# A second level of Strassen's form inside three of the seven aggregation products of a graph layer

## The chip, the core and the metric

The kernel runs on one core of one Trainium2 chip. The metric is device time in microseconds (us) of one execution; lower is better. Engines are named as the profile names them: PE is TensorE (matmuls), PEld its weight loads, DVE is VectorE, ACT is ScalarE, POOL is GpSimd, and SP is SyncE, which here only issues DMAs.

## The reference

Two graph layers over `x` (8 batches, 2048 nodes, 256 features) and one matrix `adj` (2048 x 2048), all in fp32. The change lies in the first product of the first layer, `agg`:

```python
# layer 0
A_norm = adj + eye(2048)
dinv = rsqrt(A_norm.sum(0) + A_norm.sum(1) - diagonal(A_norm))
A_hat = A_norm * dinv[:, None] * dinv[None, :]
agg = einsum('nm,bmd->bnd', A_hat, x)              # 8 x 2048 x 256
h = relu(batchnorm(agg.reshape(-1, 256) @ W1.T + b1))   # 256 -> 512
out = batchnorm(h @ W2.T + b2)                     # 512 -> 256
x = layernorm(x + out)
# layer 1: attention with 4 heads, masked where adj == 0
q, k, v = split(x @ W)
x = layernorm(x + softmax(q @ k.T / 8 + mask) @ v)
```

## The kernel before

**Aggregation as seven products.** Let A be `adj` plus the identity, turned so that the contracted node lies on the partitions. Columns of A are cut into chunks of 512 output nodes: `k` (0 or 1) names a pair of chunks, one in each half of the nodes. For one `k`, `T[k, (i, j)]` is the block of contracted half i and output half j, held as 128 x 8 x 512 (8 blocks of 128 contracted nodes). On the other side `S[v, i, j]` is `x` of batch b+i, contracted half j, and 128 of the 256 features (`d` is 0 or 1), held as 128 x 8 x 128. Two batches by two halves times two halves by two halves is a 2 x 2 block product. It is done in Winograd's variant of Strassen's form, with seven products in place of eight. The sums and differences of operands are called `S[v, 1]` to `S[v, 4]` (functions `s1` to `s4`) and `T[k, 2]` to `T[k, 4]` (`t2` to `t4`); `T[k, (0, 1)]` is overwritten with its own difference to `T[k, (0, 0)]`.

**Units.** The loop at L453 runs over 16 units `v = (k, b, d)`: two k, four pairs of batches, two halves of the features. A unit is seven calls of `product` (L360), each of 8 matmuls of 128 x 128 weights by 512 columns into one of four PSUM buffers of pool `psa`. The order on PE is p1, p6, p2, p7, p4, p5, p3. Each product is read from PSUM and added into a quarter of `ag` (tiles ag00, ag10, ag11, ag01; the first index is the batch, the second the half of output nodes); p1 is copied by ScalarE, the others are added by VectorE, and each finished quarter is multiplied by `dbc` (dinv of the output nodes) on GpSimd.

**What goes beside it.** While unit v runs, the next unit's `S` tiles are loaded by SP (`load_form`, L169), multiplied by dinv on GpSimd (`scale`, L333) and combined on GpSimd (`s1` to `s4`). The tiles are called forms; class `Form` hands out nine names, and `product` gives the name back after its last use. At the turn from k=0 to k=1 new `T` blocks are fetched from scratch memory, and VectorE makes the mask of zeros (`mask_of`, L186), `T[k, (0, 1)]`'s difference and t2 to t4.

**Linear layer.** After both d of a pair of batches, `linear` (L404) multiplies `ag` of one batch by W1, again with seven products (PSUM pool `psh`, matmul L412). Their operands `G[i, 1]` to `G[i, 4]` come from `linear_form` (L402) on GpSimd, partly in place in `ag`. Results go into tiles h0 and h1, then to scratch memory `h_d`, and VectorE takes batch norm statistics of them. `linear` for batch 1 of the pair follows the unit directly; for batch 0 it is put into a list `later`, which is run in the next unit just after p1.

**Order.** The whole stage is under a manual schedule: each engine executes its instructions in the order in which the Python code issues them. An instruction that waits holds up everything behind it on its engine.

**After it** come the last four chunks' linear layer (L678), the second linear layer (L633), and attention (L945 to L986), which takes most of the span.

Of the kernel before, what the change touches and what calls it, by code (L numbers as in the profile page):

```python
# [26 lines left out]
def tile_gcn_then_masked_attention(  # L27
# [102 lines left out]

    HT = NT // 2
    NK = HT // TPC
    CHUNKS = ((0, 0), (1, 0), (1, 1), (0, 1))
# [18 lines left out]
        T[1, ij] = quarter(4 + s)  # L154


    free = [f"x{i}" for i in range(9)]

    class Form:
        def __init__(self):  # L160
# [6 lines left out]
    def load_form(b, j, d):  # L167
        f = Form()
        nc.sync.dma_start(  # L169
            f.t,  # L170
            x[b, j * HT * P : (j + 1) * HT * P, d * P : (d + 1) * P].rearrange(
                "(t p) d -> p t d", p=P
            ),
        )
        return f

    def mask_out(k, ij, m8):
        i, j = ij
        c0 = (j * NK + k) * CH
        nc.sync.dma_start(mask_d[:, i * HT : (i + 1) * HT, c0 : c0 + CH], m8)  # L180

    def mask_of(k, ij):

        i, j = ij
        m8 = bp.tile([P, HT, CH], U8, name="m8")
        nc.vector.tensor_scalar(m8, T[k, ij], 0.0, None, op0=ALU.is_equal)  # L186
        if i == j:
            for q in range(TPC):
                m = k * TPC + q
                nc.vector.tensor_copy(  # L190
                    m8[:, m, q * P : (q + 1) * P], mdiag[:, i * HT + m, :]
                )
        mask_out(k, ij, m8)
# [4 lines left out]
    with tc.tile_pool(name="bt7", bufs=1, side="right") as bp7, tc.tile_pool(  # L198
# [4 lines left out]
        engines=ALL4  # L203
    ):
        T[1, HALVES[3]] = quarter(7, bp7)
        m8 = bp.tile([P, HT, CH], U8, name="m8")
        rsum = sp1.tile([P, NT], F32, name="rsum")
        diag = sp1.tile([P, NT], F32, name="diag")

# [87 lines left out]
        diagonal()  # L297
        first_t1(nc.vector, slice(2 * P, CH))
        mask_out(0, (0, 1), m8)

    lp = right.enter_context(
        tc.tile_pool(name="l0", bufs=1, side="right", reuse_waits="tile")
# [1 line left out]
    with tc.tile_pool(  # L304
        name="psa", bufs=4, space=PSUM
    ) as psa, tc.tile_pool(name="psh", bufs=4, space=PSUM) as psh, tc.manual_schedule(engines=ALL4):
        for j in range(2):
            lp.tile([P, NH, CH], F32, name=f"h{j}")
        w1f = lp.tile([P, 4, H // 2], F32, name="w1f")
        dbc = []  # L310

# [48 lines left out]
        def product(s, t):  # L360
            pa = psa.tile([P, CH], F32, name="pa")
            for m in range(HT):
                nc.tensor.matmul(  # L363
                    pa, s.t[:, m, :], t[:, m, :], start=(m == 0), stop=(m == HT - 1)
                )
            s.done()
            return pa
# [5 lines left out]
        def t3(k, slot):  # L373
            T[k, 3] = quarter(slot)
            nc.vector.tensor_sub(T[k, 3], T[k, 2], T[k, (0, 0)])
# [5 lines left out]
        def fetch(k, ij, slot):  # L381
            T[k, ij] = quarter(slot)
            nc.sync.dma_start(T[k, ij], bt_d[HALVES.index(ij)])
# [20 lines left out]
        def linear(k, b, ag, i):  # L404

            cs = [(b + i) * NCH + j * NK + k for j in range(2)]
            lo, hi = (lp.tile([P, NH, CH], F32, name=f"h{j}") for j in range(2))

            def products(w, t):
                for s in range(2):  # L410
                    ph = psh.tile([P, CH], F32, name="ph")
                    nc.tensor.matmul(ph, W1[w][:, s * P : (s + 1) * P], t, start=True, stop=True)  # L412
                    yield s, ph

            def plus(h, f, p, u):
                nc.vector.scalar_tensor_tensor(
                    h[:, f, :], p, b1s[:, f : f + 1], u, op0=ALU.add, op1=ALU.add
                )

            for s, p in products((0, 0), ag[i, 0][:, 0, :]):  # L420
                nc.scalar.copy(lo[:, 2 + s, :], p)  # L421
            linear_form(ag, i, 3)
            for s, p in products((0, 1), ag[i, 0][:, 1, :]):
                plus(lo, s, p, lo[:, 2 + s, :])
            linear_form(ag, i, 4)
            for s, p in products(2, G[i, 2]):
                nc.vector.tensor_add(hi[:, s, :], p, lo[:, 2 + s, :])
            for s, p in products(3, G[i, 3]):
                nc.vector.tensor_add(hi[:, 2 + s, :], p, hi[:, s, :])
            for s, p in products((1, 1), G[i, 4]):  # L430
                plus(lo, 2 + s, p, hi[:, 2 + s, :])
            nc.sync.dma_start(h_d[cs[0]], lo)
            for s, p in products(1, G[i, 1]):
                plus(hi, 2 + s, p, hi[:, 2 + s, :])
                nc.vector.tensor_add(hi[:, s, :], p, hi[:, s, :])
            for s, p in products(4, ag[i, 1][:, 1, :]):
                plus(hi, s, p, hi[:, s, :])
            nc.sync.dma_start(h_d[cs[1]], hi)
            for c, h in zip(cs, (lo, hi)):
                for f in range(NH):  # L440
                    nc.vector.bn_stats(st1[:, f, c, :], h[:, f, :])

        later = []
        for i, j in ((0, 0), (1, 0), (1, 1), (0, 1)):
# [4 lines left out]
        nc.gpsimd.tensor_sub(W1[2], W1[1], W1[0, 0])  # L449
        nc.gpsimd.tensor_sub(W1[3], W1[0, 0], W1[1, 0])  # L450
        nc.gpsimd.tensor_sub(W1[4], W1[0, 1], W1[2])
        ag = None
        for v, (k, b, d) in enumerate(units):  # L453
            first, last = v == 0, v == len(units) - 1
# [6 lines left out]
            c11, c12, c21, c22 = (ag[ij][:, d, :] for ij in HALVES)  # L461
            u1, u2, u3 = c21, c12, c22

            def do_p6():
                p6 = product(S[v, 2], T[k, 2])
                nc.vector.tensor_add(u2, p6, u1)

            p1 = product(S[v, 0, 0], T[k, (0, 0)])
            for f in later:
                f()  # L470
            later = []
            nc.scalar.copy(u1, p1)  # L472
            if not last:
                nb, nd = units[w][1:]
                S[w, 0, 0] = load_form(nb, 0, nd)
                S[w, 1, 0] = load_form(nb + 1, 0, nd)
                S[w, 1, 1] = load_form(nb + 1, 1, nd)
            if turn:
                fetch(k + 1, (0, 0), 0)
            if first:  # L480
# [4 lines left out]
                t4(0, 6)  # L485
            else:
                do_p6()
            if turn:
                fetch(k + 1, (0, 1), 4)
            p2 = product(S[v, 0, 1], T[k, (1, 0)])  # L490
            nc.vector.tensor_add(c11, p2, u1)  # L491
            nc.gpsimd.tensor_mul(c11, c11, dbc[0][:, 0, :])  # L492
            if first:
                p3 = product(S[v, 4], T[k, (1, 1)])
                do_p6()
            if not last:
                S[w, 0, 1] = load_form(nb, 1, nd)
                for ij in ((0, 0), (1, 0), (1, 1)):
                    scale(w, *ij)
            if turn:  # L500
                fetch(k + 1, (1, 1), 2)
            if d and not last:
                for i in range(2):
                    linear_form(ag, i, 1)
            p7 = product(S[v, 3], T[k, 3])
            nc.vector.tensor_add(u3, p7, u2)
            if turn:
                mask_of(k + 1, (0, 1))
                t1 = T[k + 1, (0, 1)]
                nc.vector.tensor_sub(t1, t1, T[k + 1, (0, 0)])  # L510
            if not (last or turn):
                s1(w)
                s2(w)
                s3(w)
            p4 = product(S[v, 1, 1], T[k, 4])
            nc.vector.tensor_add(c21, p4, u3)
            nc.gpsimd.tensor_mul(c21, c21, dbc[0][:, 0, :])
            if turn:
                fetch(k + 1, (1, 0), 6)
                t2(k + 1, 5)  # L520
            if not last:
                scale(w, 0, 1)
                if not turn:
                    s4(w)
            p5 = product(S[v, 1], T[k, (0, 1)])
            nc.vector.tensor_add(c22, p5, u3)
            nc.vector.tensor_add(u2, p5, u2)
            nc.gpsimd.tensor_mul(c22, c22, dbc[0][:, 1, :])
            if d and not last:
                linear_form(ag, 1, 2)  # L530
            if turn:
                t3(k + 1, 1)
            if not first:
                p3 = product(S[v, 4], T[k, (1, 1)])
            nc.vector.tensor_add(c12, p3, u2)
            nc.gpsimd.tensor_mul(c12, c12, dbc[0][:, 1, :])

            n = v % (len(units) // NK)
            if n in (2, 4, 6):
                mask_of(k, ((0, 0), (1, 0), (1, 1))[n // 2 - 1])  # L540
            if last:
                break
            if d:
                linear(k, b, ag, 1)
                linear_form(ag, 0, 2)
                if turn:
                    t4(k + 1, 3)
                    s1(w)
                    s2(w)
                later = [lambda k=k, b=b, ag=ag: linear(k, b, ag, 0)]  # L550
                if turn:
                    later += [lambda w=w: s3(w), lambda w=w: s4(w)]

# [13 lines left out]

        x0 = []  # L570
        for name, size in (
            ("h1", [P, NH, CH]), ("dbc", [P, 2, CH]), ("w1f", [P, 4, H // 2])
        ):
            t = lp.tile(size, F32, name=name).rearrange("p a b -> p (a b)")
            for i in range(size[1] * size[2] * 2 // N):
                tx = t[:, i * N // 2 : (i + 1) * N // 2].rearrange("p (t d) -> p t d", d=D)
                nc.sync.dma_start(
                    tx, x[0, len(x0) * CH : (len(x0) + 1) * CH].rearrange("(t p) d -> p t d", p=P)
                )
                x0.append(tx)  # L580
        wt = lp.tile([P, NH, CH], F32, name=f"h0")
        w2s = wt[:, :2, :].rearrange("p a b -> p (a b)").rearrange("p (f o) -> p f o", f=NH)
        w2f = wt[:, 2:, :].rearrange("p a b -> p (a b)").rearrange(
            "p (n f o) -> p n f o", n=4, f=2
        )
        nc.sync.dma_start(w2s, w2t.rearrange("(c p) f -> p c f", p=P))
        for n, slot in enumerate((0, 5, 6, 1, 3)):
            read_h(2 + n, slot)

        def w_half(i, j):  # L590
            return w2s[:, 2 * j : 2 * j + 2, i * P : (i + 1) * P]

        W = {ij: w_half(*ij) for ij in HALVES}
        W[1], W[2], W[3], W[4] = (w2f[:, n] for n in range(4))
        nc.gpsimd.tensor_add(W[1], W[1, 0], W[1, 1])
        nc.gpsimd.tensor_sub(W[2], W[1], W[0, 0])
        nc.gpsimd.tensor_sub(W[3], W[0, 0], W[1, 0])
# [753 lines left out]
```

## Time and profile before

| | |
|---|---|
| Median of 3 runs | 3564.32 us (3564.18 to 3565.26) |
| Profiled execution | 3566.12 us, its span 3564.3 us |
| Mean granted PE clock | 0.998 |
| Busy share of the span | PE 99%, DVE 59%, ACT 44%, POOL 65% |
| First and last matmul of the aggregation (L363) | 58.9 and 999.5 us |
| Aggregation matmuls (L363), 1792 records | 774.8 us busy |
| Linear layer inside the stage (L412), 392 records | 76.8 + 76.7 + 26.3 us busy |

Every fp32 matmul shows as two records, so 16 units of seven products of 8 matmuls are 1792 records. A record's duration includes the pipeline: records start closer together than they last, so the pace is read from the starts and not from the mean duration. Busy times of one group are unions and can be added up along one engine.

### The profile page before, as it was taken

The numbers are of one execution on the slowest core, as the hardware profiler recorded it, in microseconds if no ns is written. First come the engines' busy times: TensorE is split into PE (matmuls) and PEld (weight loads), VectorE is DVE, ScalarE is ACT, GpSimd is POOL, SyncE is SP. The second block draws the span as 40 slices with busy tenths as digits, with TensorE's granted clock in tenths as the row PEclk, the third lists the DMA queues.
The fourth block names the chain that finished last, engine by engine and source line by source line (L and its number), as shares of the span: only waits on it lengthen the run. The fifth ranks groups of instructions, "written<-read, shape, count | busy, mean of one in ns | idle before, by whom it ended". The sixth has DMA issues, their size and how long they took to land. (4 is left out here: it accounts for less than half of the span.)

```text
span 3564.3 us, 55375 instructions
## 1 busy us (share of the span) xinstructions
PE 3527.1 (99%) x22483; PEld 1461.0 (41%) x22483; DVE 2113.4 (59%) x3128; ACT 1575.4 (44%) x1952; POOL 2330.5 (65%) x1588
## 2 busy tenths in 40 slices
PE   8999999999999999999999999999999999999998
PEld 5444444444444433433343433343443334343332
DVE  6224343442346656766766776676676676677666
ACT  5000000000045455665665565565566566566555
POOL 4544364435357656777777787777677777777777
PEclk9999999999999999999999999999999999999999
DMA  9122342231256445666575566566656556555655
GB/s 342 54 77 76 95 153 78 71 95 39 84 217 249 156 84 109 128 126 123 110 149 117 115 129 134 113 133 129 118 124 136 114 117 145 115 117 115 122 107 121
DMA packets 197577, 440.16 MB, mean 123 GB/s; under 512 B 14128, under 2 KB 121152, under 8 KB 186944
## 3 DMA queue, kind: packets, MB, share of 16 engines
q0 software_dynamic: 64656, 239.37, 35.3%
q1 hardware_dynamic: 132048, 196.11, 16.2%
q8 instruction: 178, 2.92, 0.3%
q10 hardware_dynamic: 608, 1.06, 0.1%
q14 instruction: 87, 0.71, 0.1%
HBM read 126.62 MB, written 75.51 MB: 57 GB/s over the span
## 5 line engine op out<-in xcount | busy, mean ns | idle before, releaser
L945 DVE SCALAR_TENSOR_TENSOR prob<-mask,st 128x1024 f32<-128x1024 uint8 x1024 | 1239.0, 1215 | 434.6 <-PE st L933 358.6
L951 ACT ACTIVATE prob<-prob 128x1024 f32<-128x1024 f32 x1024 | 1081.2, 1056 | 913.4 <-DVE prob L945 836.6
L963 PE MATMUL out_ps<-prob,v 64*64 64x512 f32 x8192 | 1074.2, 595 | 3.6 <-DVE ot L991 2.6
L933 PE MATMUL st<-qt,kt 64*64 64x512 f32 x8192 | 1062.9, 589 | 0.1
L986 POOL TENSOR_TENSOR acc<-acc,prob 128x1024 f32<-128x1024 f32 x317 | 825.6, 2604 | 5.5 <-DMA prob<-prob 0.6
L363 PE MATMUL pa<-t,x 128*128 128x512 f32 x1792 | 774.8, 594 | 2.8 <-ACT t L239 2.8
L973 POOL DMA_DIRECT2D prob<-prob x447 | 403.6, 928 | 565.4 <-PE out_ps L963 453.4
L933 PEld LDWEIGHTS st<-qt,kt 64*64 64x64 f32 x8192 | 312.5, 133 | 566.7 <-issue 527.0
L363 PEld LDWEIGHTS pa<-t,x 128*128 128x128 f32 x1792 | 341.4, 191 | 432.9 <-issue 428.7
L963 PEld LDWEIGHTS out_ps<-prob,v 64*64 64x64 f32 x8192 | 290.8, 133 | 542.4 <-issue 470.5
L975 POOL TENSOR_TENSOR acc<-acc,prob 128x1024 f32<-128x1024 f32 x126 | 298.1, 2366 | 7.5
L867 PE MATMUL pm<-x1t,wq 128*128 128x512 f32 x512 | 250.8, 613 | 0.7 <-ACT x1t L836 0.7
L492 POOL TENSOR_TENSOR ag<-ag,dbc 128x512 f32<-128x512 f32 x16 | 20.2, 1264 | 314.7 <-DVE ag L491 287.2
L472 ACT COPY ag<-pa 128x512 f32<-128x512 f32 x16 | 9.4, 588 | 450.0 <-PE pa L363 434.0
L421 ACT COPY h<-ph 128x512 f32<-128x512 f32 x28 | 16.4, 585 | 416.7 <-PE ph L412 416.7
L984 POOL TENSOR_TENSOR acc<-prob 128x1024 f32<-128x1024 f32 x64 | 170.7, 2667 | 3.0 <-DMA prob<-prob 3.0
L762 ACT ACTIVATE x<-x,ln_nm,ln_rs 128x256 f32<-128x256 f32 x256 | 137.6, 586 | 7.5 <-POOL ln_nm L758 7.5
L1039 DVE SCALAR_TENSOR_TENSOR x<-pm,ri,x 128x64 f32<-128x64 f32 x512 | 109.6, 277 | 43.6 <-PE pm L1031 43.6
L867 PEld LDWEIGHTS pm<-x1t,wq 128*128 128x128 f32 x512 | 86.9, 189 | 118.2 <-issue 111.6
L881 PE MATMUL pm<-wq,x1t 128*128 128x128 f32 x1024 | 125.1, 275 | 0.0
L881 PEld LDWEIGHTS pm<-wq,x1t 128*128 128x128 f32 x1024 | 119.4, 192 | 2.5 <-ACT x1t L836 1.7
L991 DVE TENSOR_TENSOR ot<-out_ps,ot 128x512 f32<-128x512 f32 x64 | 44.3, 692 | 123.9 <-ACT ot L990 123.9
(158 smaller groups left out, 2863.5 us busy)
## 6 DMA issues: line engine op xcount, KB each, us to landing
prob<-prob POOLq DMA_DIRECT2D x447, 512.0 KB, 4.9
x<-in_x_dram SPq DMA_DIRECT2D x92, 512.0 KB, 6.5
h_d<-h SPq DMA_DIRECT2D x28, 1024.0 KB, 4.3
t<-h_d SPq DMA_DIRECT2D x28, 1024.0 KB, 8.2
a<-in_adj_dram SPq DMA_DIRECT2D x16, 1024.0 KB, 5.4
y_d<-ag SPq DMA_DIRECT2D x32, 512.0 KB, 2.7
out_dram<-x SPq DMA_DIRECT2D x31, 512.0 KB, 6.6
yt<-y_d SPq DMA_DIRECT2D x28, 512.0 KB, 3.3
```

Of the source, the lines that this page charges most:

```text
L363: nc.tensor.matmul(pa, s.t[:, m, :], t[:, m, :], start=(m == 0), stop=(m == HT - 1))
L762: nc.scalar.activation(self.t[:, i, :], self.t[:, i, :], AF.Identity, bias=self.nm[:, i : i + 1], scale=self.rs[:, i : i + 1],)
L867: nc.tensor.matmul(pm, wq[:, d, wcols], xt[:, d, cols], start=(d == 0), stop=(d == ND - 1))
L881: nc.tensor.matmul(pm[:, j * P : (j + 1) * P], xt[:, d, t * P : (t + 1) * P], wq[:, d, wcols], start=(d == 0), stop=(d == ND - 1),)
L933: nc.tensor.matmul(st[r * HD : (r + 1) * HD, h, :], kt[hs, j * P + r * HD : j * P + (r + 1) * HD], qt[hs, cols], start=True, stop=True,)
L945: nc.vector.scalar_tensor_tensor(p, mask[:, j, cols][:, None, :].to_broadcast([P, 2, CH]), MASKED, st, op0=ALU.mult, op1=ALU.add,)
L951: nc.scalar.activation(probs[g], probs[g], AF.Exp)
L963: nc.tensor.matmul(outs[u][hs, r, :], inp.qkv[b, hp][2][rs, j, hs], probs[g][rs, h, :], start=(j == 0), stop=(j == NT - 1),)
L973: nc.gpsimd.dma_start(probs[g - 1], probs[g], accum_op=ALU.add)
L975: nc.gpsimd.tensor_add(accs[u], accs[u], probs[g])
L984: nc.gpsimd.tensor_add(accs[v], probs[g - 7], probs[g - 5])
L986: nc.gpsimd.tensor_add(accs[v], accs[v], probs[g - 5])
```

## The change

Products p4, p5 and p3 are no longer done once per unit. p1, p6, p2 and p7 stay as they are in both units of a pair. After p7 of the second unit, each of p4, p5, p3 is done for both halves of the features at once, as a 2 x 2 block product of its own: two halves of features by two halves of the contracted 8 blocks, times two halves of those by two halves of the 512 columns. Class `Inner` does it with seven inner products of 4 matmuls of 256 columns. Its sums and differences are made by GpSimd on the side of x (`s12`, `s3`, `s4`, results in four tiles `narrow0` to `narrow3`) and by VectorE on the side of A (`t2`, `t3`, `t4`, in two tiles `wide0` and `wide1`). Results are put together in a form `sums` and then added to the quarters of `ag` (`targets`). `by_rows` multiplies a quarter of `ag` by `dbc` for both halves of the features.

The tiles h0 and h1 of `linear` become the same two wide and four narrow tiles, stored in six DMAs instead of two. There are ten forms instead of nine, since three of the first unit's are kept for the inner products. Masks are built in `wide0`, in a form at the turn. The three blocks used inside get their own difference in place (three subtractions at the first pair of each k). The first unit's p3, which stood ahead of its p6, goes. Loads, scales and s1 to s4 of the next unit are issued at other places:

```diff
-    free = [f"x{i}" for i in range(9)]
+    free = [f"x{i}" for i in range(10)]
...
+            def t2(self):
+                self.y2 = self.place_t(self.e)
+                nc.vector.tensor_sub(self.y2, self.b(1, 1), self.b(0, 1))
+            def t3(self):
+                self.y3 = self.place_t(1 - self.e)
+                nc.vector.tensor_sub(self.y3, self.y2, self.b(0, 0))
+            def t4(self):
+                nc.vector.tensor_sub(self.y2, self.b(1, 0), self.y2)
+            def s12(self):
+                self.x1, self.x2 = self.place_s(0), self.place_s(1)
+                nc.gpsimd.tensor_add(self.x1, self.a(1, 0), self.a(1, 1))
+                nc.gpsimd.tensor_sub(self.x2, self.x1, self.a(0, 0))
+            def s3(self):
+                self.x3 = self.place_s(2)
+                nc.gpsimd.tensor_sub(self.x3, self.a(0, 0), self.a(1, 0))
+            def s4(self):
+                self.x4 = self.place_s(3)
+                nc.gpsimd.tensor_sub(self.x4, self.a(0, 1), self.x2)
+            def run(self, place, follower=None, extra=()):
...
+                def product(s, t):
+                    p = psa.tile([P, CH], F32, name="pa")[:, :H2]
+                    for m in range(M):
+                        nc.tensor.matmul(
+                            p, s[:, m, :], t[:, m, :], start=(m == 0), stop=(m == M - 1)
+                        )
+                    return p
+                p1 = product(self.a(0, 0), self.b(0, 0))
+                nc.scalar.copy(c21, p1)
+                p2 = product(self.a(0, 1), self.b(1, 0))
+                nc.vector.tensor_add(c11, p2, c21)
+                more()
+                p6 = product(self.x2, self.y2)
+                self.t4()
+                nc.vector.tensor_add(c12, p6, c21)
+                p5 = product(self.x1, self.b(0, 1))
+                more()
+                if follower:
+                    follower.s12()
+                p7 = product(self.x3, self.y3)
+                nc.vector.tensor_add(c22, p7, c12)
+                nc.vector.tensor_add(c12, p5, c12)
+                if follower:
+                    follower.t2()
+                    follower.s3()
+                p4 = product(self.a(1, 1), self.y2)
+                nc.vector.tensor_add(c21, p4, c22)
+                nc.vector.tensor_add(c22, p5, c22)
+                more()
+                p3 = product(self.x4, self.b(1, 1))
+                nc.vector.tensor_add(c12, p3, c12)
+                for dst, src in self.targets:
+                    nc.vector.tensor_add(dst, c, src)
+                more()
+                if follower:
+                    follower.t3()
+                    follower.s4()
...
             def do_p6():
                 p6 = product(S[v, 2], T[k, 2])
                 nc.vector.tensor_add(u2, p6, u1)
+                if not d:
+                    for ij in ((0, 0), (1, 0), (1, 1)):
+                        scale(w, *ij)
+                    s1(w)
+                elif not last:
+                    load(1, 0)
...
             nc.gpsimd.tensor_mul(c11, c11, dbc[0][:, 0, :])
             if first:
-                p3 = product(S[v, 4], T[k, (1, 1)])
                 do_p6()
+            if not d:
+                s2(w)
+                scale(w, 0, 1)
+            elif not (last or turn):
+                load(1, 1)
...
+                inner[0].t2()
+                inner[0].t3()
+                inner[0].s12()
+                inner[0].s3()
+                inner[0].s4()
             p7 = product(S[v, 3], T[k, 3])
             nc.vector.tensor_add(u3, p7, u2)
+            if not d:
+                s3(w)
+                s4(w)
+                n = v % (len(units) // NK) // ND
+                if n < 3:
+                    mask_of(k, ((1, 1), (0, 0), (1, 0))[n], wide(0))
+                if n == 0:
+                    for tk in (4, (0, 1), (1, 1)):
+                        t = inner_t(k, tk, 0, 1)
+                        nc.vector.tensor_sub(t, t, inner_t(k, tk, 0, 0))
+                continue
...
+            inner[0].run(sums.t, inner[1], extra[:4])
+            if turn:
+                load(1, 1)
+            if not last:
+                load(0, 1)
+            by_rows((1, 0), 0)
+            if turn:
+                fetch(k + 1, (1, 0), 6)
+            elif not last:
+                s1(w)
+                s3(w)
+            inner[1].run(sums.t, inner[2], extra[4:8])
+            by_rows((1, 1), 1)
+            if not last:
+                linear_form(ag, 1, 1)
+                linear_form(ag, 1, 2)
+                if turn:
+                    scale(w, 1, 1)
+                scale(w, 0, 1)
             if not (last or turn):
+                s2(w)
+                s4(w)
+            inner[2].run(sums.t, None, extra[8:])
+            sums.done()
+            if last:
+                by_rows((0, 1), 1)
+                break
+            linear(k, b, ag, 1)
+            by_rows((0, 1), 1)
+            linear_form(ag, 0, 1)
+            linear_form(ag, 0, 2)
+            later = [lambda k=k, b=b, ag=ag: linear(k, b, ag, 0)]
+            if turn:
                 s1(w)
                 s2(w)
...
+                later += [lambda f=f, w=w: f(w) for f in (s3, s4)]
+                later += [lambda k=k: t3(k + 1, 1), lambda k=k: t4(k + 1, 3)]
```

At the turn, `extra` holds ten pieces that `more()` hands out one at a time: two slices of the new mask, four of the new `T[1, (0, 1)]` and four of `T[1, 2]`. After the loop, x of batch 0 and W2 are loaded into the new wide and narrow tiles instead of h0 and h1.

## The prediction

> **What bounds the kernel now.** I read the page's busy shares and slices first, then the busy time by stretch, the groups by shape, and the timeline of a few engines. The page:
>
> ```profile
> PE 3527.1 (99%) x22483; PEld 1461.0 (41%) x22483; DVE 2113.4 (59%) x3128; ACT 1575.4 (44%) x1952; POOL 2330.5 (65%) x1588
> ...
> PE   8999999999999999999999999999999999999998
> ...
> POOL 4544364435357656777777787777677777777777
> ```
>
> TensorE is never short of work. The aggregation runs from 59 to 1000 us, and the stretches inside it are full:
>
> ```profile
> 60.00:100.00 40.00, 40.00 (x90) 17.43 (x89) 20.20 (x10) 8.30 (x28) 12.25 (x12) 0.94 0.73 264
> ...
> 300.00:400.00 100.00, 100.00 (x235) 44.27 (x234) 26.14 (x37) 1.23 (x3) 50.20 (x29) 1.00 0.24 69
> ```
>
> The columns are the length, the busy time (and count) of PE, PEld, DVE, ACT and POOL, then the granted clock, the DMA share and GB/s. In the second row PE is full, VectorE has 26 of 100 us and GpSimd 50. So PE time removed here is end time removed, as long as no other engine takes over. The groups by shape give the prices:
>
> ```profile
> L363 PE MATMUL pa<-t,x 128*128 128x512 f32 x1792 | 774.8, 594 | 2.8 <-ACT t L239 2.8
> ...
> L333 POOL TENSOR_TENSOR x<-x,dinv 128x1024 f32<-128x1024 f32 x60 | 112.5, 1896 | 0.0
> ...
> L346 POOL TENSOR_TENSOR x<-x,x 128x1024 f32<-128x1024 f32 x15 | 35.2, 2345 | 0.6
> ...
> L402 POOL TENSOR_TENSOR ag<-g,ag 128x512 f32<-128x512 f32 x14 | 19.4, 1385 | 93.6 <-PE ph L412 93.6
> ```
>
> L402 is `linear_form`: today GpSimd waits there for PE (93.6 us), never the reverse. The timeline of PE gives the pace of matmuls at two widths:
>
> ```profile
> 410.63 7.03 PE L363 MATMUL pa<-t,x 128*128 128x512 f32 x16
> ...
> 1244.70 1.95 PE L881 MATMUL pm<-wq,x1t 128*128 128x128 f32 x16
> ```
>
> Each matmul is two records. At 512 columns: (7.03 - 0.592)/15 = 0.429 us a record, 6.86 us a product. At 128 columns with full weights: (1.95 - 0.275)/15 = 0.112 us, so weights can be changed every 0.112 us. Last, VectorE and GpSimd side by side where k turns:
>
> ```profile
> 507.19 4.88 DVE L371 TENSOR_TENSOR t<-t,t 128x4096 f32<-128x4096 f32 x1
> ...
> 507.76 5.45 POOL L517 TENSOR_TENSOR ag<-ag,dbc 128x512 f32<-128x512 f32 x1
> ...
> 513.17 1.90 POOL L333 TENSOR_TENSOR x<-x,dinv 128x1024 f32<-128x1024 f32 x1
> ...
> 513.32 6.03 DVE L375 TENSOR_TENSOR t<-t,t 128x4096 f32<-128x4096 f32 x1
> ...
> 515.02 5.45 POOL L528 TENSOR_TENSOR ag<-ag,dbc 128x512 f32<-128x512 f32 x1
> ```
>
> The 512-element multiply takes 1.26 us alone. Here it takes 5.45, ending 1.14 us after the subtraction on VectorE does; that subtraction takes 4.42 us alone and 6.03 when it finds L333 running. They take turns.
>
> **What the Trainium skill says.** "SBUF — State Buffer", section "Who interferes with whom": a VectorE instruction with two SBUF inputs contends with a GpSimd instruction that reads SBUF, and the second to come waits for the whole of the first. The lines above agree; evictions (PSUM and SBUF input) stay at 0.69 us beside GpSimd, as the page has it too. "TensorE: Matmul & The Clock Gate", part 1: an idle window of 3413 ns halves the clock. The trace has it once: after PE's 2.76 us gap at 56 us the clock is 0.94 in the first stretch above. "VectorE: DVE Perf Modes", the errata section, gives (N+151)/0.96 ns for an fp32 tensor_tensor: 1.224 us at 1024 elements, where L358 took 1.22.
>
> **The change, part by part.** I count in pairs of units (d = 0, 1), eight of them.
>
> *PE.* Before: 14 products x 6.86 + two `linear` of 28 records x 0.429 (12.0) = 120.1 us. After: 8 x 6.86, plus 21 inner products of 8 records at 256 columns, plus 24.0. No row has 256 columns with full weights: half of 0.429 is 0.2145, and 0.112 for weights is below it. Bounds 0.2145 and 0.24; I take the first. 21 x 1.716 = 36.0, sum 114.9: **5.15 us saved a pair, 41.2 in all**.
>
> *VectorE.* Added per inner group: t2, t3, t4 (1024 elements, 1.22), seven evictions of 256 (0.42, estimated as 0.69 less 256/0.96 ns), one to two target adds of 1024 (1.22): 7.8 to 9.0 us in 12. It fits, but 13 of these per pair (nine t, four targets) have two SBUF inputs and take turns with GpSimd. Removed: eight 512 evictions. One turn, from the lines above: the handovers overlap by about 0.13 us each, so 1.22 - 0.26 + 0.03 = 0.97 us.
>
> *GpSimd.* Added: x1 to x4, twelve operations of 512, 1.23 us start to start. More important is where they stand. Let 0 be p1 of d=0. On PE follow `linear` of row 0, p6, p2, p7, p1', p6', p2', which ends at 60.0; p7' to 66.9; 36.0 of inner products to 102.9; then `linear` of row 1, whose fourth product (G3) is due 3 x 1.72 later, at **108.1**. G3 is made by the third `linear_form` on GpSimd, in order behind: c11's multiply (it waits for p2', so it starts at 60.95), 12 x operations, 4 `by_rows`, two `linear_form`s, 4 scales, s1, s3, s2, s4. With itself: 20 x 1.23 + 4 x 1.87 + 4 x 2.33 = 41.4, and some 0.7 for operations that wait for the one just before. Alone it would be ready at 103.1, 5 us early. With the 13 turns (12.6) it is ready at **115.7**, plus 0.2 to PE: PE waits 7.8 us, some of it earlier, in inner group 3's p6, which waits for x2 (about 2.6), and 4 to 5 us before G3. Pair: 114.9 + 7.8 = 122.7, **+2.6**.
>
> *Turn pair (k 0 to 1).* s1 to s4 move behind `linear`, 9.3 us less ahead of G3; two mask slices and eight slices of t1, t2 come, ten more turns, 9.7. Same within 0.5.
>
> *First pair.* d=0 has now four products, so p1' is due at 89.6 in the trace's time, where seven covered the start before. But its operand is scaled behind c11's multiply, which waits for dbc:
>
> ```profile
> 93.30 1.26 POOL L492 TENSOR_TENSOR ag<-ag,dbc 128x512 f32<-128x512 f32 x1 [27.59 <-DMA dbc<-dinv_d]
> 94.52 5.60 POOL L333 TENSOR_TENSOR x<-x,dinv 128x1024 f32<-128x1024 f32 x3
> ```
>
> Then three scales, s1, s2 to 104.9, and three turns for the in-place subtractions: p6', due at 96.5, starts at 107.8: +11.3. With 7.8 and -5.15: **+14.0**.
>
> *First pair of k=1.* t3 and t4 (4.42 each) and the mask of (1,1) now lie beside scale, s1, s2 of the next unit: 0 to 6 us late at p6'; I take 3.
>
> *Last pair.* No next unit to prepare: -5.15.
>
> *Costed at nothing:* h_d stores in six pieces instead of two (four more SP issues of 0.35 ahead of the x loads; these have 10 us before scale is due); x loads one at a time; mask stores from wide0 and from a form (the store, 3.7 us, has 13 us until t2); x0 and w2 loads at the end (27 us of L678 matmuls cover them). If that cover goes, the few us show before the first L633. ScalarE's copy of p1 is idle-engine work.
>
> *Clock.* Seven gaps of 4 to 5 us hold a whole 3.41 us window about 4 times in 10; each drop costs 2 to 3 us (the first stretch above lost 0.06 of 40). +6, bounds 0 and 21 (all seven, 3 each).
>
> **Sum:** 14.0 + 6 x 2.6 + 3 - 5.15 + 6 = +33. The profiled execution took 3566.12 (span 3564.3, 1.8 around it), 1.8 above the median of the runs, 3564.32; I add the difference to the median: **3598**.
>
> **Rivals.** *PE stays the bound.* If the turns cost less (short operations slip in where the other engine waits for a semaphore anyway), GpSimd is on time and 41.2 is kept but for the first pair's 11.3 and about 1: **3535**. It decides at a turn's price: the sum is about -62 + 91 x price, zero at 0.68 us. For it: GpSimd alone has 5 us to spare, and the turns seen are with 4096-element operations. Against: in my order GpSimd has hardly a wait between 61 and 116, so what VectorE takes is lost; L346 on VectorE (1024 elements, 65.3 us) took 1.53 behind a GpSimd operation. *The clock drops in every gap:* 21 in place of 6, **3613**. *Narrow matmuls don't run at half price:* at 0.24 us a record the 1344 records give 34 of the 41 us back; but GpSimd sets the seven pairs' end then as well, so only the last pair loses: about **3602**. That fewer products are issued is plain from the loops.
>
> **How the numbers follow.** Turns bind: 0.55 (own range 3578 to 3622). PE stays the bound: 0.28. Clock in every gap 0.08, narrow matmuls dear 0.03, in between (some turns hidden) 0.06. The 8-in-10 range runs from 3535, the middle of the fast case, to 3622. 0.2% (7 us) is about what a measurement of this kernel tells from no change. Faster 0.28, same 0.06, slower 0.66.
>
> **What would show it.** Right: PE idle of some 7 us a pair, mostly before L412 products and released by GpSimd's `linear_form`; GpSimd nearly without idle in d=1; GpSimd 512 operations with a mean well above 1.26; the 1024-element subtractions on VectorE above 1.22; a PE gap near 90 us. Wrong: aggregation PE at 100% and pairs of 115 us; narrow records not at 0.215 us apart; the time going to evictions that hold PSUM.

## The result, and the profile after

The changed kernel takes 3594.31 us (median of 4 runs, 3592.16 to 3597.69), the kernel before 3564.25 us in the same runs: ratio 1.0086, 95% interval 1.0074 to 1.0098. It is slower by 30 us. Its profiled execution took 3592.16 us with a span of 3590.4 us, 26.1 us more than the span before.

The page of the changed kernel, busy shares and the slices of PE and GpSimd:

```profile
PE 3507.4 (98%) x23059; PEld 1578.7 (44%) x23059; DVE 2354.1 (66%) x3349; ACT 1584.4 (44%) x1976; POOL 2537.1 (71%) x1684
...
PE   8899999999999999999999999999999999999998
...
POOL 3956676676558647777777777777777777777777
```

PE is busy for 20 us less than before and yet the span is longer: time has turned from work into waits. VectorE is busy for 241 us more and GpSimd for 207, part of it time in which one holds up the other. The same two stretches by engine (length, busy PE, PEld, DVE, ACT, POOL, clock, DMA share, GB/s):

```profile
60.00:100.00 40.00, 33.26 (x73) 14.16 (x72) 31.76 (x17) 8.12 (x28) 15.10 (x13) 0.91 0.75 277
300.00:400.00 100.00, 98.82 (x294) 55.49 (x292) 54.58 (x70) 2.99 (x6) 60.31 (x32) 1.00 0.28 85
```

The first stretch lost 7 us of PE to the first pair. In the second, VectorE's share has doubled. Whom PE waits for is in the waits of PE (total us, times, longest):

```profile
PE ph L429 <- POOL ag L417: 15.1, 6, 2.6
PE pa L532 <- POOL narrow L510: 14.4, 6, 2.4
...
PE pa L378 <- POOL x L348: 6.0, 1, 6.0
PE pa L532 <- DVE wide L499: 4.5, 2, 3.2
PE pa L532 <- DVE wide L502: 3.3, 2, 2.4
```

L417 is `linear_form`, L510 makes x2, L348 is `scale`; L499 and L502 are the inner t3 and t4. Before, it was GpSimd that waited for PE at `linear_form`. The third pair on PE's timeline, from its p1 (304.08) to the next one's (426.48), with most of its rows left out:

```profile
304.08 7.03 PE L378 MATMUL pa<-t,x 128*128 128x512 f32 x16
...
415.08 1.88 PE L429 MATMUL ph<-g,w1f 128*128 128x512 f32 x4
419.51 1.98 PE L429 MATMUL ph<-ag,w1f 128*128 128x512 f32 x4 [2.55 <-POOL ag L417]
...
426.48 7.03 PE L378 MATMUL pa<-t,x 128*128 128x512 f32 x16
```

The pair takes 122.40 us. Before it was 120.17, from the p1 at 290.46 to the one at 410.63:

```profile
290.46 7.03 PE L363 MATMUL pa<-t,x 128*128 128x512 f32 x16
```

The bracket is the idle time just before a row and what ended it: the product that uses G3 waited 2.55 us. Inside the inner products the wait for x2 looks like this:

```profile
395.20 3.62 PE L532 MATMUL pa<-t,x 128*128 128x256 f32 x16
401.22 3.26 PE L532 MATMUL pa<-wide,narrow 128*128 128x256 f32 x8 [2.40 <-POOL narrow L510]
404.27 2.36 PE L532 MATMUL pa<-t,narrow 128*128 128x256 f32 x8
406.47 1.89 PE L532 MATMUL pa<-wide,narrow 128*128 128x256 f32 x8
```

Eight records of 256 columns take 1.89 us at full clock, and 3.26 just after the gap: the clock was halved. GpSimd at the same time, and VectorE's inner t3 and targets:

```profile
396.72 2.24 POOL L509 TENSOR_TENSOR narrow<-x 128x512 f32<-128x512 f32 x1
399.05 2.12 POOL L510 TENSOR_TENSOR narrow<-narrow,x 128x512 f32<-128x512 f32 x1
401.13 2.24 POOL L514 TENSOR_TENSOR narrow<-x,x 128x512 f32<-128x512 f32 x1
403.34 1.26 POOL L518 TENSOR_TENSOR narrow<-x,narrow 128x512 f32<-128x512 f32 x1
...
418.19 1.26 POOL L417 TENSOR_TENSOR ag<-g,ag 128x512 f32<-128x512 f32 x1
```

```profile
395.86 4.18 DVE L562 TENSOR_TENSOR ag<-x,ag 128x1024 f32<-128x1024 f32 x2
399.97 2.28 DVE L499 TENSOR_TENSOR wide<-wide,t 128x1024 f32<-128x1024 f32 x1
```

A GpSimd operation of 512 elements takes 1.26 us, or 2.24 where a VectorE operation with two SBUF inputs came in between: 0.98 us is the price of one turn (0.97 was forecast). In this pair thirteen operations on GpSimd from c11's multiply to G3 are lengthened in this way, by 0.86 to 1.05 us, 12.4 us together. VectorE pays too: 2.28 in place of 1.22. The last line of GpSimd is the maker of G3: it ends at 419.45, 115.4 us after the pair's p1.

### The profile page after: what moved, and what is told of

It is laid out like the page before. It is cut to its first block, busy times and chain, and to the rows that moved or that the text cites. A ratio compares the mean times of both kernels' runs of the same rounds, so it can differ in the third digit from the quotient of the medians.

```text
span 3590.4 us, 57093 instructions
## 1 busy us (share of the span) xinstructions
PE 3507.4 (98%) x23059; PEld 1578.7 (44%) x23059; DVE 2354.1 (66%) x3349; ACT 1584.4 (44%) x1976; POOL 2537.1 (71%) x1684
## 5 line engine op out<-in xcount | busy, mean ns | idle before, releaser
L1130 DVE SCALAR_TENSOR_TENSOR prob<-mask,st 128x1024 f32<-128x1024 uint8 x1024 | 1238.7, 1215 | 434.8 <-PE st L1118 359.7
L378 PE MATMUL pa<-t,x 128*128 128x512 f32 x1024 | 445.4, 595 | 11.4 <-POOL x L348 6.0
L378 PEld LDWEIGHTS pa<-t,x 128*128 128x128 f32 x1024 | 194.9, 191 | 258.7 <-issue 241.5
L348 POOL TENSOR_TENSOR x<-x,dinv 128x1024 f32<-128x1024 f32 x60 | 128.1, 2156 | 104.1 <-DMA x<-in_x_dram 104.1
L538 ACT COPY x<-pa 128x256 f32<-128x256 f32 x24 | 8.9, 372 | 391.9 <-DVE ag L562 215.1
L1176 DVE TENSOR_TENSOR ot<-out_ps,ot 128x512 f32<-128x512 f32 x64 | 44.2, 691 | 123.9 <-ACT ot L1175 123.9
```

The source lines that it names most:

```text
L378: nc.tensor.matmul(pa, s.t[:, m, :], t[:, m, :], start=(m == 0), stop=(m == HT - 1))
L1130: nc.vector.scalar_tensor_tensor(p, mask[:, j, cols][:, None, :].to_broadcast([P, 2, CH]), MASKED, st, op0=ALU.mult, op1=ALU.add,)
```

## The experiments

**1. Is it the second SBUF input, or just VectorE's work?** The control gives up one PSUM buffer of the linear layer for a tile of zeros. The experiment puts this tile in place of one SBUF operand of the inner t operations: same engine, order, element and instruction count, but one SBUF input. Each operation then leaves out one of its operands, so the kernel does not compute the layer; only its time is read.

```diff
# control (pool psh gets bufs=3 in place of 4, and a new pool psz one buffer)
+        zero = psz.tile([P, CH], F32, name="zero")
+        nc.vector.memset(zero, 0.0)
# experiment, on top of it (zeros() is that tile, broadcast to 4 x 256)
-nc.vector.tensor_sub(self.y2, self.b(1, 1), self.b(0, 1))
+nc.vector.tensor_sub(self.y2, zeros(), self.b(1, 1))
-nc.vector.tensor_sub(self.y3, self.y2, self.b(0, 0))
+nc.vector.tensor_sub(self.y3, zeros(), self.y2)
-nc.vector.tensor_sub(self.y2, self.b(1, 0), self.y2)
+nc.vector.tensor_sub(self.y2, zeros(), self.b(1, 0))
```

> The changed kernel with one of the linear layer's four PSUM buffers given up for a constant tile of zeros that nothing reads: the control for the next kernel. Every theory: 3594 us, up to 5 us more if three buffers hold up the linear layer's products. Pairs of units 122.4 us from p1 to p1, as in the changed kernel.

Measured: 3596.77 us, 2.5 more than the changed kernel.

> Changed part of the computation: the nine t subtractions of a pair on VectorE take the tile of zeros in PSUM in place of one of their two SBUF operands, so as many elements, as many instructions and the same order, but one SBUF input. Shared-port theory: nine of thirteen turns go, 9 x 0.97 = 8.7 us, G3 is ready at 106.7 after p1 and on time (108.1), ordinary pairs fall from 122.4 to about 115.0, seven pairs: 3594 - 52 = about 3540 us, and GpSimd's 512-element operations go back to 1.27 us outside the four target adds. Rival, VectorE's amount of work or late evictions hold PSUM: same as the control within 5 us, since VectorE issues the same work. Rival, GpSimd's own amount of work: same as the control.

Measured: 3549.21 us, 47.6 less than the control; ratio to the kernel before 0.9960 (0.9946 to 0.9975). The groups by shape of this kernel (x4, x1 and t3), then of the changed one (t3 and x1):

```profile
L525 POOL TENSOR_TENSOR narrow<-x,narrow 128x512 f32<-128x512 f32 x24 | 36.7, 1528 | 12.1 <-PE pa L539 12.1
...
L516 POOL TENSOR_TENSOR narrow<-x 128x512 f32<-128x512 f32 x24 | 31.5, 1314 | 19.4 <-PE pa L539 19.4
...
L506 DVE TENSOR_TENSOR wide<-zero,wide 128x1024 f32<-128x1024 f32 x24 | 29.2, 1215 | 0.3
```

```profile
L499 DVE TENSOR_TENSOR wide<-wide,t 128x1024 f32<-128x1024 f32 x24 | 52.8, 2201 | 0.3
...
L509 POOL TENSOR_TENSOR narrow<-x 128x512 f32<-128x512 f32 x24 | 45.8, 1910 | 6.0 <-PE pa L532 5.9
```

x1 falls from a mean of 1910 to 1314 ns, and t3 from 2201 to 1215. So neither the number of operations on VectorE nor that on GpSimd, both unchanged, made the loss: the second SBUF input did, by the turns that it forces. It fell short of the 52 to 54 us expected. Ordinary pairs took 116.8 us and not 115.0: GpSimd, now early, waits for PE at x1 and x4 (19.4 and 12.1 us over the stage), G3 was ready at 109.8 after p1 in the third pair and not at 106.7, and PE still waits 1.3 us before it:

```profile
PE ph L433 <- POOL ag L421: 8.1, 6, 1.4
```

**2. Is it what stands ahead of G3?** s1 to s4 of the next unit go behind the linear layers for every pair.

```diff
-            elif not last:
-                s1(w)
-                s3(w)
             inner[1].run(sums.t, inner[2], extra[4:8])
...
-            if not (last or turn):
-                s2(w)
-                s4(w)
             inner[2].run(sums.t, None, extra[8:])
...
+            s1(w)
+            s2(w)
+            later += [lambda f=f, w=w: f(w) for f in (s3, s4)]
             if turn:
-                s1(w)
-                s2(w)
-                later += [lambda f=f, w=w: f(w) for f in (s3, s4)]
```

> s1, s2 of the next unit are issued behind the linear layer of batch 1 and s3, s4 behind that of batch 0 for every pair, as the changed kernel does at the turn only. Theory (GpSimd, with VectorE's turns, makes G3 too late): 9.3 us less ahead of G3, which is ready at 106.1 after p1, on time; PE's waits before G3 and before x2 go and with them the clock drops; ordinary pairs 115.0, six pairs gain 7.4 each: about 3550 us, the turn pair stays. Rival, evictions by VectorE or PSUM buffers hold PE: within 5 us of 3594. Rival, what is moved is late at its new place (s2 for p6 of the next pair): waits of PE for x at p6, pairs above 118, 3570 or more.

Measured: 3548.40 us; ratio to the kernel before 0.9957 (0.9940 to 0.9973). The third pair takes 115.34 us:

```profile
288.31 7.03 PE L378 MATMUL pa<-t,x 128*128 128x512 f32 x16
...
396.79 1.88 PE L429 MATMUL ph<-ag,w1f 128*128 128x512 f32 x4
...
403.65 7.03 PE L378 MATMUL pa<-t,x 128*128 128x512 f32 x16
```

The product with G3 has no idle time ahead of it, and GpSimd waits for PE at the maker of G3, as it did in the kernel before:

```profile
393.66 1.27 POOL L417 TENSOR_TENSOR ag<-g,ag 128x512 f32<-128x512 f32 x1 [1.30 <-PE ph L429]
```

GpSimd does the same 44 operations in this pair as in the changed kernel, but the four that were moved no longer stand ahead of what PE needs; eleven turns fall ahead of G3 where thirteen did. With this one move of four operations the second level of Strassen's form pays: 16 us less than the kernel before, of the 41 that PE saves.

**3. Does the order ahead of G3 matter, or only the sum?** s1 and s3 are moved from the first gap between inner groups to just ahead of s2 and s4: the wait for x2 should go and the one before G3 grow by as much.

```diff
-            elif not last:
-                s1(w)
-                s3(w)
...
             if not (last or turn):
-                s2(w)
-                s4(w)
+                for f in (s1, s3, s2, s4):
+                    f(w)
```

> From the changed kernel, s1 and s3 of the next unit move from between the first and second inner group to just ahead of s2 and s4; all four still stand ahead of G3. Chain theory (the sum of GpSimd's work and VectorE's turns ahead of G3 sets the pair, not where PE waits first): PE's wait for x2 (2.4 us a pair) and the clock drop behind it go, the wait before G3 grows from 2.5 to about 6.5 us, ordinary pairs stay at 122.4 within 0.7 (a clock drop behind G3 instead could add up to 1.7), total 3594 within 8. Rival, the wait for x2 and the clock drop it causes are losses of their own: about 4 us a pair less, 3570.

Measured: 3606.83 us, 12.5 more than the changed kernel, where at most 8 were expected. In its third pair:

```profile
416.22 1.88 PE L429 MATMUL ph<-g,w1f 128*128 128x512 f32 x4
425.31 3.50 PE L429 MATMUL ph<-ag,w1f 128*128 128x512 f32 x4 [7.21 <-POOL ag L417]
```

The wait for x2 is gone and the one before G3 is 7.21 us. G3 ends at 425.25, 115.8 us after p1 (309.44); in the changed kernel it was 115.4. So the sum sets the moment, not the order. What the expectation had wrong is the clock: after 7.2 us of idle time it is halved and stays so, four records take 3.50 us in place of 1.88, and the stretch from there to the next p1 takes 8.5 us instead of 7.0. The pair is 124.4 us long, the other pairs with this wait 125.0 to 125.8. A clock drop costs nothing where PE has to wait later anyway (as after x2 in the changed kernel), and its full price where it stands last.

**4. The first pair.** In the first unit the scales and s1 are put ahead of c11's multiply.

```diff
-            nc.gpsimd.tensor_mul(c11, c11, dbc[0][:, 0, :])
             if first:
                 do_p6()
+            nc.gpsimd.tensor_mul(c11, c11, dbc[0][:, 0, :])
```

> In the first unit alone, GpSimd scales the next unit's x and makes s1 ahead of c11's multiply, which waits for dbc. Theory: p1 of the second unit no longer waits 6 us for its scale, the clock drop behind it goes, part comes back as a wait for s2 at p6 (up to 4 us): 4 to 8 us less, about 3588 us. Rival, the x loads land no earlier than dbc does: no change, 3594.

Measured: 3590.40 us, 3.9 less than the changed kernel's median; single runs of the two overlap (3586.87 to 3592.43 against 3592.16 to 3597.69), so the total alone is not clear. The profile is clear: the first pair takes 118.1 us in place of 123.0, and the second unit's p1 no longer waits for a scale. Two scales now run at 65.17, long before c11's multiply; the third waits for its x until 88.70:

```profile
65.17 5.71 POOL L348 TENSOR_TENSOR x<-x,dinv 128x1024 f32<-128x1024 f32 x2
88.70 1.89 POOL L348 TENSOR_TENSOR x<-x,dinv 128x1024 f32<-128x1024 f32 x1 [17.82 <-DMA x<-in_x_dram]
```

Little of these 4.9 us shows in the total of this execution (its span is 1.6 us shorter): two ordinary pairs took 123.9 and 123.8 us with a second clock drop, and the turn pair 127.2.

**5. Both, and the turn.** The edits of 2 and 4 together; and in a second kernel also the four slices of T[1, 2] taken out of the inner products at the turn.

```diff
-                extra += [lambda m=m: t2_slice(m) for m in range(0, HT, 2)]
...
             linear(k, b, ag, 1)
+            if turn:
+                t2(k + 1, 5)
```

> s1 to s4 behind the linear layer for every pair and, in the first unit, the scales ahead of c11's multiply. If the two are independent, as the theory has them (other pairs, other waits): 3548.4 - 3.9 = about 3544 us. If the first pair's gain was only a shorter clock drop that the second edit had removed already: 3548.

Measured: 3543.30 us, where 3544 was expected of two independent edits. They add up: the first pair takes 109.7 us (115.0 with edit 2 alone).

> The same, and at the turn the four slices of T[1, 2] leave the inner products for one whole subtraction behind the linear layer of batch 1. Theory for the turn pair: there VectorE is the engine that PE waits for (wide from L499 and L502, 7 us), since each of its two-input operations waits for one of GpSimd's; four fewer of them between the inner products take 4 to 8 us off, and the clock drop of 10 us in the turn pair gets shorter: turn pair from 128 to 120 to 124 us, total about 3538 us. Rival, the turn pair is bound by fetches of T blocks or by x: no change from the kernel beside it.

Measured: 3537.20 us, ratio to the kernel before 0.9925 (0.9911 to 0.9938). The turn pair fell from 125.8 us (the kernel beside it) to 119.7; in the six traces that have the old code there, with its t operations, it took 125.5 to 128.1. PE's waits between the inner products, in the kernel beside it and then in this one:

```profile
PE pa L532 <- DVE wide L502: 4.7, 2, 2.4
PE pa L532 <- DVE wide L499: 3.3, 2, 2.0
...
PE pa L532 <- DVE wide L502: 2.4, 1, 2.4
PE pa L532 <- DVE wide L499: 1.3, 1, 1.3
```

4.3 us of waits went, and with them the one clock drop of this pair, 3.4 us at half clock. This version beats both kernels, the one before by 27 us. Of the 41 us that PE was to save some 14 are still missing. The turn pair and the first pair keep about half of it: they are 4 and 3 us short of the 4.9 that the last pair saves.

## Why the prediction came out as it did

The forecast was 3598 us (range 3535 to 3622) and slower at 0.66; measured 3594.3. By its steps:

- **PE saves 5.15 us a pair: right.** The last pair, which has nothing to wait for, is 103.2 us long instead of 108.1: 4.9 less. Its 168 inner records take 36.3 us from the first one's start to the start of what follows, 0.216 us a record where half the pace of 512 columns is 0.2145. At the rival's 0.24 they would take 40.3 us; that rival is out.

```profile
988.53 3.62 PE L532 MATMUL pa<-t,x 128*128 128x256 f32 x16
...
1024.79 5.74 PE L863 MATMUL ph<-ag,w1s 128*128 128x512 f32 x13
```

- **Turns cost 0.97 us, G3 is ready at 115.7: right,** 0.98 and 115.4. The rival that stays PE-bound needed a price below 0.68. Experiment 1 shows the turns as the cause, experiment 2 the place ahead of G3.
- **Ordinary pair +2.6:** 2.2 in each of the four (122.3 to 122.4 against 120.2). The wait for x2 was 2.4 us (2.6 forecast), the one before G3 only 2.5 (4 to 5 forecast), since PE reached it late, after 3.4 us at half clock.
- **First pair +14.0:** 11.65. The mechanism was right, and p1' waited 5.95 us for `scale`. But dbc landed by 90.2 us and not 93.3, and p6' started at 103.95 and not 107.8.
- **Turn pair "same within 0.5": wrong.** It was +4.8. The step counted what the turns do to GpSimd and not what they do to VectorE. There a two-input operation first waits for one of GpSimd's (2.2 us in place of 1.22), and at the turn ten more of VectorE's operations that take turns stand between the inner products (the two mask slices, 1.22 and 1.96 us, among them). PE then waits for t3 and t4 on VectorE, 7.8 us, and not for G3. Taking four out (experiment 5) cut the pair by 6.1 us.
- **First pair of k=1 +2.6 and 3:** 4.8, against 5.6.
- **Clock +6: wrong in its mechanism, 3 us in size.** The step had a gap bring a drop only if it holds a whole window of 3.41 us. Its own example, the gap at 56 us, is 2.76 us long. In the profiled execution a drop followed the 2.4 us wait for x2 in all six pairs that have it. There it cost nothing, because G3 is ready when GpSimd says so: where no drop came at that place (the first pair of the control and of experiment 4), the wait before G3 was 4.1 and 4.2 us. Two pairs, the first of each k, had a second drop, behind the wait for G3. Their `linear` took 16.5 us from start to end in place of 15.0, so these drops cost 3 us. Which pairs get this second drop is chance: in the control and in experiment 4 ordinary pairs got it (124.0, 123.9 and 123.8 us). Experiment 3 shows both sides of it.

With 3 us for the clock the forecast's sum is +30.5; the span grew by 26.1, of which 25.0 lie in the aggregation. The profiled execution is the lowest of the four runs. By the spans the forecast of +33 is 7 us too high, by the medians (+30.0) it is 3. That it came so close is in part luck: the 2.2 us that the turn pair cost beyond its forecast are set off by the 2.4 us that the first pair cost less. What makes the other three runs 2 to 5 us longer is not shown; their clock is 0.992 where the profiled one has 0.993, and other traces with the same code have longer turn pairs and more second drops. The term that decided, 13 turns on GpSimd ahead of one `linear_form`, was right to 0.3 us.

The Trainium skill's section "Who interferes with whom" of "SBUF — State Buffer" says that a VectorE instruction with two SBUF inputs contends with a GpSimd instruction that reads SBUF, and that one with at most one SBUF input, outside modes that it names, does not. Experiment 1 agrees: 2201 against 1215 ns for the same operation. That it is a shared port, as the section has it, no run here shows by itself. The skill's free-running window of 3413 ns ("TensorE: Matmul & The Clock Gate", part 1) is found in these traces as a grid on which drops begin, but PE need not be idle for the whole of it, as the last section shows.

## What to carry to other kernels

Before an edit that trades matmuls for elementwise work, add GpSimd's time and VectorE's two-SBUF-input time between the last thing they wait for and the next thing PE needs, as if the two were one engine, which is what the turns made of them here; compare this sum with PE's time over the same stretch, not over the whole stage. If it is too long, first look for operations in that queue which are needed only later: moving four of them was worth 46 us here. Count the turns on both engines, since either can be the one that PE waits for.

## What the runs showed of the hardware

**When the clock halves.** Each drop in the clock record of the nine traces begins on a grid of its own execution: the drops of one trace begin a whole number of 3.413 us apart, to 0.01 us. Where this grid lies in the kernel differs from execution to execution. Below are the changed kernel's third pair on its grid, around the gap for x2 and around the one before G3, and the gap of the kernel before (columns as above: length, busy PE, PEld, DVE, ACT, POOL, clock, DMA share, GB/s):

```profile
398.39:401.80 3.41, 1.01 (x5) 0.56 (x5) 3.41 (x2) 0.37 (x1) 3.33 (x3) 1.00 0.00 0
401.80:405.21 3.41, 3.41 (x10) 2.70 (x9) 1.48 (x3) 0.00 (x0) 3.41 (x3) 0.50 0.00 0
415.46:418.87 3.41, 1.50 (x4) 0.38 (x2) 2.02 (x3) 0.00 (x0) 3.33 (x3) 1.00 0.38 154
418.87:422.28 3.41, 2.77 (x7) 1.34 (x8) 1.38 (x2) 0.00 (x0) 3.41 (x4) 1.00 0.00 0
...
54.82:58.23 3.41, 1.31 (x12) 1.07 (x10) 2.99 (x6) 1.18 (x3) 2.56 (x2) 1.00 1.17 294
58.23:61.64 3.41, 2.74 (x4) 1.22 (x5) 1.73 (x1) 3.41 (x13) 3.41 (x3) 0.50 0.85 188
```

The gap of 2.40 us falls into one window of the grid, in which PE is idle for 2.40 of 3.41 us, and the next window has half clock. The gap of 2.55 us is cut by the grid into 1.91 and 0.64, and no drop follows. This holds throughout: from 50 to 1050 us of the nine traces a drop followed each of the 50 windows at full clock in which PE was idle for 2.05 us or more, and none of the 2511 with 2.01 us or less. Later in the kernel six drops followed 1.90 to 1.99 us, so the limit is about 2 us of a window as this profile counts idle time. From 50 to 1050 us a drop lasted until a window in which PE was idle for at most 0.57 us, which can take more than one: behind the gaps of 7.2 us in experiment 3 it began inside the gap in all six pairs and lasted 6.8 to 10.2 us.
